# One transformer block on one core: another order, a VectorE minimum and other copies in the last attention stage

## The chip, the cores and the metric

The kernel runs on one core of one Trainium2 chip. The metric is the device time of one execution in microseconds (us). Three executions of the kernel before took 1998.77 to 1999.62 us, with a median of 1999.25 us.

Five engines have their own queue of instructions each and work through it in order: TensorE (PE in the profile, its weight loads PEld), VectorE (DVE), ScalarE (ACT), GpSimd (POOL) and SyncE (SP), which here only starts DMAs. Semaphores tie them together. TensorE writes to PSUM, which has eight banks of 128 partitions x 512 float32; VectorE and ScalarE read and write both PSUM and SBUF, and GpSimd works in SBUF.

## What is computed

The input is 2048 tokens of 512 numbers. It is normalised (layer norm without weights) to xn, and the output is x + attention(xn) + ffn(xn):

```python
xn = _layernorm(x)                       # (1, 2048, 512)
q, k, v = split(xn @ w_qkv.T)            # 16 heads of 32
scores = q @ k.T / sqrt(32)
scores = where(causal, scores, lowest)
attn = softmax(scores) @ v
x1 = attn @ w_o.T
gate, up = xn @ Wg.T, xn @ Wu.T          # 4096 wide, 4-bit weights with scales
out = x + x1 + (gelu_tanh(gate) * up) @ Wd.T
```

## The kernel before

The tokens are split into four blocks of 512 queries; `ORDER = (1, 2, 3, 0)` is the order in which they are worked on. The 16 heads make 8 pairs. All matmuls but a few are in float32.

Attention is done twice over. First, `score_rows` and `maxima` compute scores with queries on the partitions and take each query's maximum; `split` cuts the negated maximum into three bfloat16 parts. `rows_from_parts` transposes them on TensorE (L269) and ScalarE copies them, so that they lie along the free dimension. Second, `score_cols` (L288) writes the negated maxima into a PSUM tile with keys on the partitions, `add_scores` (L303) adds the scores on top, and ScalarE takes the exponential, which cannot exceed one. `attend` (L351) multiplies the exponentials with the values and with a tile of ones, so that the upper half of a PSUM bank holds the values' sum and the lower half the sum of the exponentials.

A step is one block of queries against one tile of 128 keys: 4 * qb + 4 steps for block qb, 40 for a pair (`steps`). The last four key tiles of a block are diagonal: only the columns from `c0` on are computed (512, 384, 256, 128 of them), and the first 128 of those hold scores of later keys, which may exceed the maximum. In `exponentials` ScalarE therefore takes Relu(-score) of these 128 columns into `clip` (L323), the exponential of the rest (L325), and the exponential of -clip for both heads at once (L327). Then GpSimd sets the later keys' exponentials to zero (L328). A step that is not diagonal has one exponential of 512 columns for each head (L317).

The score tiles lie in two pools of three banks, `ps_t` and `ps_s`; the last two banks, `ps_m`, hold the attended values, m0 and m1. For pairs 0 to 5 the first pass of a later pair runs along with the second pass of the present one. The loop at L552 to L574 does the last two pairs (6 and 7) together, and is the stage of this change: pair 6 uses `ps_t` and m0, pair 7 `ps_s` and m1. An iteration issues the score matmuls of both pairs for this step, then `attend` of both pairs for the step before, then the exponentials of this step. When a block is complete, `keep_attention` copies the values (ScalarE, L370) and the sums (VectorE, L371) of each pair out of PSUM, and `normalize_attention` takes one reciprocal of 128x128 on VectorE (L379) and one product on GpSimd (L381) in each of the next iterations.

The same loop prepares tokens for the feed-forward part. `token_rest` cuts a 128x512 piece of xn into a high part (a mask on VectorE, L539), a low part (a subtraction on GpSimd, L542), a mixed part (VectorE, L544, which waits for GpSimd) and the raised low part (ScalarE, L547, which waits for L544). Eight pieces (the first two blocks of `ORDER`) are done here, started after steps with an even key tile that is not diagonal.

After the loop comes the output projection (L750 to L779): 16 tiles of tokens, four matmuls each (L753), added by VectorE (L760) to x. The first tiles are those of block 1. Along with it, `token_rest` prepares the other two blocks, `token_high` (L732) rebuilds the high parts, and the first 4-bit weights are decoded. Its eight PSUM banks come from the pool `ps_f` (L589). Then the feed-forward part takes the rest of the time, up to the end.

The order on every engine is the order of the program text (`manual_schedule`); a pool's buffers come round in turn.

Of the kernel before, what the change touches and what calls it, by code (L numbers as in the profile page):

```python
# [67 lines left out]
SUM_SCALE = -TRUE / SPLIT  # L68

ORDER = (1, 2, 3, 0)  # L70

STEPS = NTB * (NTB + 1) * 2

# [2 lines left out]
def block_kernel(  # L76
# [34 lines left out]
    with (  # L111
# [199 lines left out]
        def exponentials(p, n, tiles):  # L311
            qb, kt = steps[n]
            c0 = max(0, kt - 4 * qb) * P
            prob = probs.tile([P, 2, TB], F32, tag="prob", name=f"prob{p}_{n}")
            if kt < 4 * qb:
                for h, ps in enumerate(tiles):
                    nc.scalar.activation(prob[:, h, :], ps, AF.Exp)  # L317
                return prob


            clip = clipp.tile([P, 2, P], F32, tag="clip", name=f"clip{p}_{n}")
            for h, ps in enumerate(tiles):
                nc.scalar.activation(clip[:, h], ps[:, c0 : c0 + P], AF.Relu, scale=-1.0)  # L323
# [3 lines left out]
            nc.scalar.activation(diag, clip, AF.Exp, scale=-1.0)  # L327
            nc.gpsimd.affine_select(  # L328
                out=diag,
                in_=diag,  # L330
                compare_op=ALU.is_ge,
                fill=0.0,
                base=0,
                pattern=[[0, 2], [1, P]],
                channel_multiplier=-1,
            )
            return prob

        avs, sums = {}, {}

        def attend(p, n, prob):

            qb, kt = steps[n]
            if kt == 0:
                turn[0] = (NTB * p + qb) % 2 if p < NP - 2 else p % 2
                avs[p, qb] = ps_m.tile([P, TB], F32, tag=f"m{turn[0]}", name=f"av{p}_{qb}")
            av = avs[p, qb]
            c0 = max(0, kt - 4 * qb) * P
            for h in range(4):
                head = 2 * p + h % 2  # L350
                nc.tensor.matmul(  # L351
                    av[D * h : D * (h + 1), c0:],
                    lhsT=v[kt // 4][:, kt % 4, D * head : D * (head + 1)] if h < 2 else ones,
                    rhs=prob[:, h % 2, c0:],
                    start=(kt == 0),
                    stop=(kt == 4 * qb + 3),
                )
            if kt == 4 * qb + 3:
                full.append((p, qb))

        full, invert = [], []
# [1 line left out]
        def keep_attention():  # L363

            p, qb = full.pop(0)
            av = avs[p, qb]
            og, half = p // 2, slice(64 * (p % 2), 64 * (p % 2 + 1))
            if p % 2 == 0:
                sums[og, qb] = sump.tile([P, TB], F32, tag="sums", name=f"sums{og}_{qb}")
            nc.scalar.copy(aT[og][qb][half], av[:64])  # L370
            nc.vector.tensor_copy(sums[og, qb][half], av[64:])  # L371
            if p % 2 == 1:
                invert.extend((og, qb, i) for i in range(4))

# [156 lines left out]
                        wo.append(t[:, k])  # L531


        lm = {}

        def token_rest(b, k, high):

            xk, (low, mixed) = xnT[b][:, k], lm[b, k]
            nc.vector.tensor_scalar(  # L539
                high.bitcast(I32), xk.bitcast(I32), HIGH, None, ALU.bitwise_and  # L540
# [3 lines left out]
            nc.vector.scalar_tensor_tensor(  # L544
                mixed, high, SPLIT, low.bitcast(F32), ALU.mult, ALU.subtract
            )
            nc.scalar.activation(low, low.bitcast(F32), AF.Copy, scale=1.0 / SPLIT)  # L547
            yield

        early = [(i, k) for i in range(2) for k in range(NK)]  # L550
        rest = iter(())
        for n in range(STEPS):  # L552
            rows_when_due(joint=True)
            two = [score_cols(NP - 2, n, ps_t), score_cols(NP - 1, n, ps_s)]
            for i in range(2):
                add_scores(NP - 2 + i, n, two[i])
            for _ in range(2):
                attend(*pending.pop(0))
            for i in range(2):
                pending.append((NP - 2 + i, n, exponentials(NP - 2 + i, n, two[i])))  # L560
            while full:
                keep_attention()
            if invert:
                normalize_attention()
            next(rest, None)
            qb, kt = steps[n]
            if early and kt < 4 * qb and kt % 2 == 0:
                i, k = early.pop(0)
                b = ORDER[i]
                lm[b, k] = [  # L570
                    turn_tile(8 * i + 2 * k + part, f"lm{b}_{k}_{part}", F32R)
                    for part in range(2)
                ]
                rest = token_rest(b, k, qkp.tile([P, TB], F32, tag=f"qk{k % 2}", name=f"hx{b}_{k}"))  # L574
                next(rest)
        while pending:
            attend(*pending.pop(0))
        while full:
# [7 lines left out]
    stage = ctx.enter_context(tc.tile_pool(name="stage", bufs=3, reuse_waits="tile"))  # L586
    gup = ctx.enter_context(tc.tile_pool(name="gu", bufs=4, reuse_waits="tile"))
    accp = ctx.enter_context(tc.tile_pool(name="acc", bufs=1, reuse_waits="tile"))
    ps_f = ctx.enter_context(tc.tile_pool(name="ps_f", bufs=8, space=PSUM))  # L589

    def bank(name):
        return ps_f.tile([P, TB], F32, tag="f", name=name)
# [136 lines left out]
    def token_high(b, k):  # L729

        xh[b, k] = late.tile([P, TB], F32R, tag=f"aT{k}_{b}", name=f"xh{b}_{k}")
        nc.vector.scalar_tensor_tensor(  # L732
            xh[b, k], lm[b, k][0].bitcast(F32), -SPLIT, xnT[b][:, k], ALU.mult, ALU.add
        )

    with tc.manual_schedule():

# [12 lines left out]
        for n, t in enumerate(order):  # L750
# [193 lines left out]
```

## Time and profile before

| what | value |
|---|---|
| median of three executions | 1999.25 us (1998.77 to 1999.62) |
| the profiled execution | 1999.17 us |
| its span, first to last instruction | 1997.4 us |
| TensorE busy | 1960.7 us (98%) |
| VectorE, ScalarE, GpSimd busy | 1311.8, 1105.3, 727.4 us |
| the last two pairs | from 734.4 us to about 859 us |
| output projection | 860.35 us to about 916 us |
| TensorE idle from 734 to 862 us | 128.0 - 117.6 = 10.4 us |
| mean granted clock of TensorE | 0.998 |

A row of the timeline has the start in us, the duration in us, the engine, the line of the kernel, the operation, the tile written <- the tiles read, the shape and the count; brackets give the idle time before it on its engine, and what ended it. A row of groups has the shape, the count, the busy time in us and the mean of one in ns, and the idle time before. TensorE's rows overlap, since it is pipelined and since matmuls that use 32 rows or columns run side by side; a step's cost is therefore read from start to start.

### The profile page before, as it was taken

The page shows a single profiled execution, that of the slowest core. Times are in us where ns is not written, and L with a number is a line of the kernel's source. Part 1 is how long each engine was busy: PE and PEld are TensorE (multiplying, and loading weights), DVE is VectorE, ACT ScalarE, POOL GpSimd, SP SyncE. Part 2 cuts the span into 40 slices and gives each one's busy share as a digit, 9 for nine tenths or more (in the row PEclk, how much of TensorE's full clock was granted, in tenths as well). Part 3 has the DMA queues.
Part 4 walks back from the last instruction along what each step waited for, and adds up shares of the span by engine and source line. Part 5 has one row for each costly group of instructions (what it writes and reads, how often), then busy time and mean ns, then how long its engine had stood idle before and what let it go on. Part 6 is the DMA issues. An engine that isn't in the chain of part 4 may idle for free.

```text
span 1997.4 us, 30985 instructions
## 1 busy us (share of the span) xinstructions
PE 1960.7 (98%) x11072; PEld 1162.0 (58%) x11072; DVE 1311.8 (66%) x2642; ACT 1105.3 (55%) x2361; POOL 727.4 (36%) x893
## 2 busy tenths in 40 slices
PE   7999999999999999999999999999999999999998
PEld 3433233333333322236888888888888888888886
DVE  5657665647565662177777777777777777767674
ACT  2112664546455668734666666666666666666664
POOL 1000110202111123154555555555555555555551
PEclk9999999999999999999999999999999999999999
DMA  3000000000000000030000000000000000000002
GB/s 127 0 11 11 1 2 1 1 12 1 1 1 12 1 1 2 1 107 21 23 21 21 20 21 21 20 21 18 23 18 23 18 23 18 23 18 22 19 5 85
DMA packets 55387, 39.79 MB, mean 20 GB/s; under 512 B 14784, under 2 KB 47552, under 8 KB 55232
## 3 DMA queue, kind: packets, MB, share of 16 engines
q1 hardware_dynamic: 55232, 37.81, 6.4%
q8 instruction: 87, 1.43, 0.3%
q14 instruction: 68, 0.56, 0.1%
HBM read 33.55 MB, written 4.19 MB: 19 GB/s over the span
## 4 chain that ended last, share of the span: by engine, by line
PE 95%; ACT 2%; DVE 1%; issue 1%; POOL 0%; DMA 0%; DVEq 0%; POOLq 0%; ACTq 0%
PE gu L796 24%; PE av L351 12%; PE gu L809 12%; PE pd L859 12%; PE ps_s L214 9%; PE ps_qk L170 6%; PE pd L871 6%; PE ps_t L288 4%; PE ps_t L303 3%; PE ps_v L450 3%; PE po L753 3%; ACT prob L317 1%; PE pm L269 1%; PE ptx L439 0%; DVE sums L371 0%
## 5 line engine op out<-in xcount | busy, mean ns | idle before, releaser
L796 PE MATMUL gu<-xh,gu 128*128 128x512 f32 x1024 | 403.9, 394 | 0.0
L796 PE MATMUL gu<-lm,gu 128*128 128x512 f32 x1024 | 403.7, 394 | 0.0
L238 DVE TENSOR_REDUCE tops<-ps_s 128x1 f32<-128x512 f32 x384 | 243.5, 681 | 157.5 <-PE ps_s L214 137.2
L880 DVE SCALAR_TENSOR_TENSOR acc<-pd,acc 128x512 f32<-128x512 f32 x512 | 316.8, 680 | 2.7 <-PE pd L871 2.7
L351 PE MATMUL av<-prob,v 128*32 128x512 f32 (+3 forms) x1280 | 290.5, 542 | 3.6 <-DVE sums L371 2.6
L214 PE MATMUL ps_s<-qk,qk 32*128 32x512 f32 (+3 forms) x1280 | 291.1, 576 | 0.0
L351 PE MATMUL av<-prob,ones 128*32 128x512 f32 (+3 forms) x1280 | 290.5, 542 | 0.0
L317 ACT ACTIVATE prob<-ps_t 128x512 f32<-128x512 f32 x384 | 205.8, 596 | 148.0 <-PE ps_t L303 146.6
L809 PE MATMUL gu<-lm,gu 128*128 128x512 f32 x1024 | 279.7, 395 | 0.0
L841 POOL TENSOR_TENSOR parts<-inter,hi 128x512 fp32r<-128x512 f32 x128 | 171.3, 1338 | 278.3 <-DVE hi L837 272.0
L833 DVE SCALAR_TENSOR_TENSOR inter<-gu,gate 128x512 f32<-128x512 f32 x128 | 88.5, 691 | 275.5 <-PE gu L809 274.1
L303 PE MATMUL ps_t<-qk,qk 32*128 32x512 f32 (+3 forms) x1280 | 264.2, 535 | 0.0
L866 ACT ACTIVATE pd<-pd 128x512 f32<-128x512 f32 x512 | 263.2, 580 | 1.1 <-PE pd L859 1.1
L859 PE MATMUL pd<-wd,parts 128*128 128x512 f32 x1024 | 259.6, 396 | 0.0
L803 ACT ACTIVATE gu<-gu 128x512 f32<-128x512 f32 x256 | 148.7, 581 | 188.2 <-PE gu L796 188.2
L809 PEld LDWEIGHTS gu<-lm,gu 128*128 128x128 f32 x1024 | 192.0, 188 | 47.1 <-issue 0.2
L796 PEld LDWEIGHTS gu<-lm,gu 128*128 128x128 f32 x1024 | 191.9, 187 | 46.6 <-POOL wd L677 0.2
L859 PEld LDWEIGHTS pd<-wd,parts 128*128 128x128 f32 x1024 | 192.3, 188 | 45.8
L796 PEld LDWEIGHTS gu<-xh,gu 128*128 128x128 f32 x1024 | 192.0, 188 | 45.7 <-ACT wd L676 0.2
L328 POOL TENSOR_SCALAR_AFFINE_SELECT prob<-prob 128x256 f32<-128x256 f32 x128 | 52.1, 408 | 423.3 <-ACT prob L327 376.7
L233 DVE CUSTOM_DVE_ANT_0 ps_s<-ps_s,mask_qk 128x128 f32<-128x128 f32 (+3 forms) x256 | 120.7, 516 | 101.5 <-PE ps_t L303 55.8
L840 ACT CAST parts<-hi 128x512 fp32r<-128x512 f32 x128 | 79.8, 623 | 172.9 <-DVE hi L837 172.9
(91 smaller groups left out, 2684.9 us busy)
## 6 DMA issues: line engine op xcount, KB each, us to landing
pk<-packed SPq DMA_DIRECT2D x96, 128.0 KB, 2.2
sc<-scales SPq DMA_DIRECT2D x512, 8.0 KB, 1.6
x<-x SPq DMA_DIRECT2D x16, 256.0 KB, 4.1
acc<-x SPq DMA_DIRECT2D x16, 256.0 KB, 3.2
sc<-scales SPq DMA_DIRECT2D x256, 16.0 KB, 1.7
out<-acc SPq DMA_DIRECT2D x16, 256.0 KB, 2.2
wqk<-w_qk SPq DMA_DIRECT2D x4, 512.0 KB, 3.6
wv<-w_v SPq DMA_DIRECT2D x4, 256.0 KB, 6.1
```

The source lines that it names most:

```text
L214: nc.tensor.matmul(ps[:, :w], lhsT=qT[p // 2, qb][rows, i * P : (i + 1) * P], rhs=kT[p // 2, c][rows, :w], start=True, stop=True,)
L238: nc.vector.tensor_reduce(top, ps[:, :w], AX.X, ALU.max)
L303: nc.tensor.matmul(ps[:, c0:], lhsT=kT[p // 2, kt // 4][rows, (kt % 4) * P : (kt % 4 + 1) * P], rhs=qT[p // 2, qb][rows, c0:], start=False ...
L317: nc.scalar.activation(prob[:, h, :], ps, AF.Exp)
L351: nc.tensor.matmul(av[D * h : D * (h + 1), c0:], lhsT=v[kt // 4][:, kt % 4, D * head : D * (head + 1)] if h < 2 else ones, rhs=prob[:, h % ...
L796: nc.tensor.matmul(ps, lhsT=parts[:, i, k], rhs=mov, start=(k == 0 and i == 0), stop=(k == NK - 1 and i == 1),)
L803: nc.scalar.activation(ps, ps, AF.Copy, scale=HIGH_SCALE)
L809: nc.tensor.matmul(ps, lhsT=gu[g, m, j][:, 2, k], rhs=lm[b, k][1], start=False, stop=(k == NK - 1), skip_group_check=True,)
L841: nc.gpsimd.tensor_tensor(parts[:, 1], inter, high, ALU.subtract)
L859: nc.tensor.matmul(po, lhsT=parts[:, part, i * P : (i + 1) * P], rhs=w[:, part], start=(part == 0), stop=(part == 1),)
L866: nc.scalar.activation(po, po, AF.Copy, scale=HIGH_SCALE)
L880: nc.vector.scalar_tensor_tensor(acc[t], po, SUM_SCALE, acc[t], ALU.mult, ALU.add)
```

## The change

It does six things, the first four of them in the stage of the last two pairs.

1. The order of the steps in this stage: the blocks come in the order 1, 0, 2, 3 (`TOGETHER`), and in block qb each of the four diagonal steps is followed by qb others. Which matmul starts and which ends a block's sum is handed to `attend`.
2. Diagonal steps: VectorE limits the 128 diagonal columns at zero, in place in PSUM, and then one exponential for each head covers all columns. The Relu and the separate exponential of the diagonal go. The zeroing on GpSimd stays.
3. When a block is complete, ScalarE copies both halves of pair 6, and VectorE both halves of pair 7.
4. Tokens of the first two blocks are prepared after even steps whose next step is not diagonal.
5. The raised low part of the tokens is taken out of `token_rest`. For the first two blocks it is made in the output projection, after the high part, which is now xn minus the unraised low part. For the other two it is issued after the mixed part as before.
6. `ps_f` gets `reuse_waits="tile"`: each of its banks waits for the earlier tiles in that place rather than for the earlier pools.

The core of the diff:

```diff
+TOGETHER = (1, 0, 2, 3)
...
-            nc.scalar.copy(aT[og][qb][half], av[:64])
-            nc.vector.tensor_copy(sums[og, qb][half], av[64:])
+            if p < NP - 2:
+                nc.scalar.copy(aT[og][qb][half], av[:64])
+                nc.vector.tensor_copy(sums[og, qb][half], av[64:])
+            else:
+                copy = nc.scalar.copy if p % 2 == 0 else nc.vector.tensor_copy
+                copy(aT[og][qb][half], av[:64])
+                copy(sums[og, qb][half], av[64:])
...
+        together = []
+        for qb in TOGETHER:
+            mine = [n for n in range(STEPS) if steps[n][0] == qb]
+            for d in range(4):
+                together += [mine[4 * qb + d], *mine[d * qb : (d + 1) * qb]]
...
+        def exponentials_together(p, n, tiles):
+            if not diagonal(n):
+                return exponentials(p, n, tiles)
+            qb, kt = steps[n]
+            c0 = (kt - 4 * qb) * P
+            prob = probs.tile([P, 2, TB], F32, tag="prob", name=f"prob{p}_{n}")
+            for h, ps in enumerate(tiles):
+
+                nc.vector.tensor_scalar(
+                    ps[:, c0 : c0 + P], ps[:, c0 : c0 + P], 0.0, None, ALU.min
+                )
+                nc.scalar.activation(prob[:, h, c0:], ps[:, c0:], AF.Exp)
+            omit_later_keys(prob[:, :, c0 : c0 + P])
+            return prob
...
-            nc.scalar.activation(low, low.bitcast(F32), AF.Copy, scale=1.0 / SPLIT)
...
-        for n in range(STEPS):
+        for s, n in enumerate(together):
...
-            qb, kt = steps[n]
-            if early and kt < 4 * qb and kt % 2 == 0:
+            if early and s % 2 == 0 and not diagonal(together[s + 1]):
...
-    ps_f = ctx.enter_context(tc.tile_pool(name="ps_f", bufs=8, space=PSUM))
+    ps_f = ctx.enter_context(
+        tc.tile_pool(name="ps_f", bufs=8, space=PSUM, reuse_waits="tile")
+    )
...
+        low = lm[b, k][0].bitcast(F32)
+        if b in ORDER[:2]:
+            nc.vector.tensor_tensor(xh[b, k], xnT[b][:, k], low, ALU.subtract)
+            multiply_low(b, k)
...
+    def multiply_low(b, k):
+        low = lm[b, k][0]
+        nc.scalar.activation(low, low.bitcast(F32), AF.Copy, scale=1.0 / SPLIT)
...
-            next(tokens, None)
+            if n in range(1, 9):
+                next(tokens)
+                multiply_low(ORDER[2 + (n - 1) // NK], (n - 1) % NK)
```

More of the change, by code (lines that the diff above doesn't have):

```diff
@@ L327, in exponentials, with omit_later_keys @@
             nc.scalar.activation(diag, clip, AF.Exp, scale=-1.0)
+            omit_later_keys(diag)
+            return prob
+        def omit_later_keys(diag):
             nc.gpsimd.affine_select(
@@ L336, in exponentials, with attend @@
             )
-            return prob
         avs, sums = {}, {}
-        def attend(p, n, prob):
+        def attend(p, n, prob, first=None, last=None):
             qb, kt = steps[n]
-            if kt == 0:
+            if first is None:
+                first, last = kt == 0, kt == 4 * qb + 3
+            if first:
                 turn[0] = (NTB * p + qb) % 2 if p < NP - 2 else p % 2
@@ L354, in attend @@
                     rhs=prob[:, h % 2, c0:],
-                    start=(kt == 0),
-                    stop=(kt == 4 * qb + 3),
+                    start=first,
+                    stop=last,
                 )
-            if kt == 4 * qb + 3:
+            if last:
                 full.append((p, qb))
@@ L531, in block_kernel, with diagonal @@
                         wo.append(t[:, k])
+        together = []
[3 more added lines that the diff above has]
+                together += [mine[4 * qb + d], *mine[d * qb : (d + 1) * qb]]
+        def diagonal(n):
+            return steps[n][1] >= 4 * steps[n][0]
+        def exponentials_together(p, n, tiles):
[10 more added lines that the diff above has]
+            omit_later_keys(prob[:, :, c0 : c0 + P])
+            return prob
         lm = {}
@@ L558, in block_kernel @@
                 attend(*pending.pop(0))
+            qb = steps[n][0]
+            ends = [
+                s == 0 or steps[together[s - 1]][0] != qb,
+                s == STEPS - 1 or steps[together[s + 1]][0] != qb,
+            ]
             for i in range(2):
-                pending.append((NP - 2 + i, n, exponentials(NP - 2 + i, n, two[i])))
+                prob = exponentials_together(NP - 2 + i, n, two[i])
+                pending.append((NP - 2 + i, n, prob, *ends))
             while full:
@@ L575, in block_kernel @@
                 next(rest)
+        assert not early
         while pending:
@@ L731, in token_high @@
         xh[b, k] = late.tile([P, TB], F32R, tag=f"aT{k}_{b}", name=f"xh{b}_{k}")
-        nc.vector.scalar_tensor_tensor(
-            xh[b, k], lm[b, k][0].bitcast(F32), -SPLIT, xnT[b][:, k], ALU.mult, ALU.add
-        )
+        low = lm[b, k][0].bitcast(F32)
+        if b in ORDER[:2]:
+            nc.vector.tensor_tensor(xh[b, k], xnT[b][:, k], low, ALU.subtract)
+            multiply_low(b, k)
+        else:
+            nc.vector.scalar_tensor_tensor(
+                xh[b, k], low, -SPLIT, xnT[b][:, k], ALU.mult, ALU.add
+            )
+    def multiply_low(b, k):
+        low = lm[b, k][0]
+        nc.scalar.activation(low, low.bitcast(F32), AF.Copy, scale=1.0 / SPLIT)
     with tc.manual_schedule():
```

## The prediction, made before the changed kernel was run

> **What bounds the kernel now.** First the page: busy shares, clock row and the chain that ended last.
>
> ```profile
> PE 1960.7 (98%) x11072; PEld 1162.0 (58%) x11072; DVE 1311.8 (66%) x2642; ACT 1105.3 (55%) x2361; POOL 727.4 (36%) x893
> ...
> PEclk9999999999999999999999999999999999999999
> ...
> PE 95%; ACT 2%; DVE 1%; issue 1%; POOL 0%; DMA 0%; DVEq 0%; POOLq 0%; ACTq 0%
> ```
>
> TensorE is busy 98% of the span and carries 95% of the chain, so a microsecond in which it stands still is a microsecond of the kernel; only 1997.4 - 1960.7 = 36.7 us are idle. The clock row rounds, so I cut the span into stretches and looked at the stage that the change touches (the last two pairs, 734.4 to 860.35 us) in pieces of 5 us. Columns: busy time with counts for each engine, then the granted clock.
>
> ```profile
> core 0: us, PE busy (x) PEld busy (x) DVE busy (x) ACT busy (x) POOL busy (x), PEclk, DMA share, GB/s
> 825.00:830.00 5.00, 5.00 (x52) 1.57 (x52) 0.00 (x0) 2.96 (x7) 0.00 (x0) 1.00 0.00 2
> 845.00:850.00 5.00, 2.81 (x40) 1.09 (x36) 0.96 (x2) 4.30 (x14) 1.22 (x3) 0.99 0.01 3
> 850.00:855.00 5.00, 5.00 (x40) 1.30 (x39) 3.82 (x5) 2.94 (x14) 1.60 (x4) 0.67 0.00 0
> 855.00:860.00 5.00, 3.19 (x52) 1.04 (x44) 1.10 (x2) 4.33 (x15) 2.52 (x7) 1.00 0.20 54
> 860.00:865.00 5.00, 4.66 (x7) 2.08 (x8) 3.68 (x5) 1.07 (x2) 1.82 (x4) 0.66 0.90 293
> ```
>
> At 825 TensorE is full. At 845 and 855 it loses 2.2 and 1.8 us, and the pieces after each run at a clock of 0.67: in pieces of 1 us this is half clock from 849.9 and from 860.4, 3.4 us each. Then the timeline of TensorE alone, for what a step costs and what it waits for.
>
> ```profile
> 758.93 0.40 PE L288 MATMUL ps_t<-neg,ones_h 3*128 3x512 bf16 x4
> ...
> 760.70 0.62 PE L288 MATMUL ps_t<-neg,ones_h 3*128 3x512 bf16 x3
> 761.90 0.37 PE L288 MATMUL ps_t<-neg,ones_h 3*128 3x512 bf16 x1 [0.59 <-ACT prob L317]
> ...
> 763.57 0.62 PE L351 MATMUL av<-prob,v 128*32 128x512 f32 x2 [0.43 <-DVE sums L371]
> ...
> 768.46 0.38 PE L288 MATMUL ps_t<-neg,ones_h 3*128 3x512 bf16 x1
> ...
> 770.18 0.37 PE L288 MATMUL ps_t<-neg,ones_h 3*128 3x512 bf16 x1 [0.58 <-ACT prob L317]
> ...
> 773.20 0.39 PE L288 MATMUL ps_t<-neg,ones_h 3*128 3x512 bf16 x4
> ...
> 776.24 0.40 PE L288 MATMUL ps_t<-neg,ones_h 3*128 3x512 bf16 x4
> ```
>
> A step of this stage is: score rows (L288, L303) for both pairs, then the values and sums (L351, "attend") of the step before. 773.20 to 776.24 is an undisturbed full step: 3.04 us. At 758.93 the attend starts 1.19 us later (760.12, next rows), so scores take 1.19 and a full attend 1.86. Narrow ones, from the same rows elsewhere: attends of 384, 256, 128 columns 1.43, 1.05, 0.58; scores 0.89, 0.65, 0.57. "x3 ... x1 <-ACT" is the score ring: three banks for a pair, two used in a step, so the fourth L288 needs the third Exp of the step before. Subtracting undisturbed durations from the start-to-start times of all 40 steps gives what the stage loses:
> - entry, 734.41 to 741.46: 0.5 + 1.5 = 2.0
> - Exps queued behind the raise of a token's low part (L547), which waits for VectorE, which waits for GpSimd (744.5, 768.5, 805.0): 1.0 + 1.7 + 1.7 = 4.4
> - a full step after a 128-column attend, then its attend waiting for the sum copy (760.70 to 765.42, again at 797): 1.7 + 1.7 = 3.4
> - diagonal steps waiting for the zeroing (L328), blocks 1 to 3: 2.0
> - block 0 at the end: 846.13 to 853.40 takes 7.27 for 2.75 of work, of which 1.7 is the half clock; with its last step 5.1
> - last attends done at 858.2, first output matmul at 860.35: 2.15, waiting for the sums
> - half clock after it, 3.4 us at half speed: 1.7
>
> Sum 20.7 us, the most that any order of this stage can give back.
>
> ```profile
> 860.35 3.98 PE L753 MATMUL po<-wo,aT 128*128 128x512 f32 x5 [1.45 <-DVE sums L371]
> ```
>
> **Part by part.** *ScalarE in diagonal steps.* Costs from the groups of this stage by shape:
>
> ```profile
> L317 ACT ACTIVATE prob<-ps_t 128x512 f32<-128x512 f32 x96 | 49.5, 601 | 15.6 <-PE ps_t L303 15.6
> ...
> L323 ACT ACTIVATE clip<-ps_t 128x128 f32<-128x128 f32 x64 | 17.6, 287 | 5.1 <-PE ps_t L303 4.5
> ...
> L327 ACT ACTIVATE prob<-clip 128x256 f32<-128x256 f32 x32 | 14.1, 442 | 0.7
> ...
> L547 ACT ACTIVATE lm<-lm 128x512 fp32r<-128x512 f32 x8 | 5.1, 644 | 7.4 <-DVE lm L544 7.4
> ...
> L233 DVE CUSTOM_DVE_ANT_0 ps_s<-ps_s,mask_qk 128x128 f32<-128x128 f32 x1 | 0.3, 295 | 0.0
> ```
>
> 64 Relus and 32 wide Exps go (17.6 + 14.1 us), and 48 narrow Exps (19.6) become 64 wider ones. In a row, an Exp advances ScalarE 0.515 us for 512 columns (2.06 for four), about 0.40, 0.29 and 0.16 for 384, 256, 128; a diagonal step of 512 columns drops from 3.0 (two pairs from 728.86 to 730.37, 1.5 each) to 2.06, below TensorE's 3.04.
>
> *VectorE's minimum, added.* 64 instructions, 128x128, PSUM to PSUM: not in the trace. Nearest row: the masked maximum above, also 128x128 in PSUM, two inputs: 295 ns. I take 0.29 us, bounds 0.2 and 0.45. [...]
>
> *Queue behind the minimum.* The built order shows VectorE's queue: minima, then reciprocals (0.93), mask (0.36) and the product waiting for GpSimd's 1.26. In most places a full step lies between and the queue is empty in time. In the entry it isn't: sum copy 739.9, two reciprocals, mask and product end at 743.5, so the second diagonal's Exps start 0.7 late (0.5 us of ring wait). In block 0 a reciprocal waits for ScalarE's copies ahead of the minima.
>
> *Raise moved out.* 8 x 0.64 us leave ScalarE here, the 4.4 us go, and come back in the output projection, where ScalarE was busy 15.7 of 50 us: nothing, as long as TensorE runs at its own pace there. High parts as a subtraction (0.68, row of L760) instead of 0.78: nothing.
>
> *Order.* TensorE's own work is unchanged. A full step after a diagonal now follows an attend of 384, 256 or 128 columns. Its third Exp ends 1.19 + 0.07 + 1.65 + 0.07 = 2.98 after its start, the next fourth L288 is reached 0.16 after the next step begins, at 2.62, 2.24, 1.77: waits 0.2, 0.58, 1.05 (the trace has this last one: 760.86 to 761.90). 1.83 per block, three blocks: 5.5, less 0.2 already in the entry: 5.3. The 3.4 and 2.0 of the ledger go.
>
> *Block 0 second.* I chain it from the durations. Last full step of block 1; diagonal 0: its Exps end 2.45 after its scores, then two copies on ScalarE, 1.19; the attend of diagonal 0 waits 0.85 for them. VectorE's reciprocal waits for the copies too, the minima of diagonal 1 follow it, ring wait 0.8. Diagonals 2 and 3: nothing. Block 2's first full step meets a 128-column attend and minima (1.38), and block 0's copies (0.6). Sum 3.65. Block 2 to 3: copies, 0.65. Copying each pair's two halves on one engine saves little: 1.19 on ScalarE against 0.58 + 0.69 in turn. The entry: 0.5 + 1.2 + 0.6 + 0.5 = 2.8; a transpose in the ring 0.2.
>
> *End.* The last step is full; its last attend runs straight into the first output matmul, which no longer waits for a whole pool: the built order shows the second projection waiting for VectorE's copies (1.4 us) behind 3.3 us of the first. 2.15 and 1.7 go. If that cover were gone, 1.4 comes back. VectorE starts the projection 2 to 3 us later against TensorE; it idled 10.2 us there for L760, so nothing.
>
> *Half clock.* [...] By the row, about 2.2 us idle in pieces within 3.4 cost 3.4 us at half clock, twice. I take the row. Block 0's new place loses at most about 1.4 idle us in such a stretch; I expect no half clock.
>
> After: 2.8 + 5.3 + 3.65 + 0.65 + 0.2 = 12.6. Gain 20.7 - 12.6 = 8.1; chaining start to start gave 7.9. I take 7.9. The profiled execution took 1999.17 (span 1997.4 and 1.8 around it), the median of the runs shown is 1999.25: 1999.2 - 7.9 = 1991.3.
>
> **Rivals.**
> - *As worked out*, 1991.3, own range 1989 to 1994: 0.55.
> - *More comes back*: the ring waits (5.3) overlap with others, 1.5 to 4 us better: 1988. For it: they are estimates of one row; against: that row is exact. 0.10.
> - *Half clock in block 0's new place and minima at 0.45*: 1.7 + 4 x 0.5 in block 0 and entry, + about 0.3: 4.0 less gain, 1995.3. For it: three waits close together. 0.17.
> - *It doesn't do what it says*: what TensorE gains up to 860 is waited for in the projection, VectorE late by 3 to 5 us at the first gate matmul: 1998.5. Against: 10.2 us of VectorE's waiting there. 0.10.
> - *Slower*: the minimum in PSUM is dear. With M per minimum, the third Exp ends about 3M + 0.17 + 0.45 after the scores, and the fourth L288 is due at 2.02; 12 diagonals lose 12 x (3M - 1.40), so the gain is eaten from M = 0.69 us. At 0.9, 12 x 1.3 = 15.6, less 7.9: 2006.9. Against: 0.295 in the nearest row. 0.08.
>
> **Numbers.** A measurement of this kernel tells about 0.2% (4 us) from no change. Below 1995.2: first two, and half of the third, and more as its size varies: 0.76; within: 0.14; slower: 0.10. Range 1988 to 1997: it leaves out the slow case, half of the fourth and a little below.
>
> **What would show it.** Right: no Exp queued behind a raise of low parts in this stage; no clock under 1 between 700 and 920; the first output matmul at about 852 to 856 with no wait; minima at 0.25 to 0.35; ring waits of about 0.6 and 1.0 after the third and fourth diagonals. Wrong: minima over 0.6; half clock near block 0; TensorE waiting for VectorE between 860 and 920; a stage that still ends near 860.

## The result and the profile after

The changed kernel takes 1991.95 us (median of 7 runs, 1990.40 to 1993.41), the kernel before, in the same comparison, 1998.77 us (7 runs, 1996.33 to 1999.62). The ratio is 0.9968, 95% interval 0.9956 to 0.9979: faster by 0.3%. The prediction was 1991.3 us, range 1988 to 1997. The profiled execution of after took 1993.41 us, its span is 1991.7.

The page of after, busy time of the engines and the shares of the chain that ended last:

```profile
PE 1958.1 (98%) x11072; PEld 1163.9 (58%) x11072; DVE 1326.4 (67%) x2706; ACT 1092.6 (55%) x2281; POOL 727.3 (37%) x893
...
PE 96%; ACT 2%; DVE 1%; issue 1%; DMA 0%; POOL 0%; DVEq 0%; SPq 0%; ACTq 0%; POOLq 0%
```

TensorE still sets the time. VectorE does 64 instructions more, ScalarE 80 fewer. The end of the changed stage, in the stretches shown of before (busy time with counts for each engine, then the granted clock):

```profile
core 0: us, PE busy (x) PEld busy (x) DVE busy (x) ACT busy (x) POOL busy (x), PEclk, DMA share, GB/s
845.00:850.00 5.00, 4.41 (x52) 1.51 (x48) 0.00 (x0) 2.59 (x7) 0.88 (x3) 1.00 0.00 2
850.00:855.00 5.00, 5.00 (x48) 1.37 (x47) 0.00 (x0) 3.92 (x8) 0.00 (x0) 1.00 0.00 0
855.00:860.00 5.00, 5.00 (x24) 1.99 (x17) 3.27 (x5) 2.77 (x5) 0.50 (x2) 1.00 0.28 65
860.00:865.00 5.00, 5.00 (x13) 2.28 (x12) 3.87 (x7) 0.03 (x1) 2.59 (x4) 1.00 0.64 198
```

The clock is 1.00 throughout; both half clocks of before (3.4 us each) are gone, and TensorE idles 0.6 us in these 20 us. The stage, from its first score row to the first output matmul, ran from 734.41 to 860.35 before (125.94 us, one half clock of 3.4 us in it) and runs from 736.16 to 856.47 now (120.31 us). What is left in it, and its end, from the timeline of TensorE:

```profile
757.89 0.40 PE L290 MATMUL ps_t<-neg,ones_h 3*128 3x512 bf16 x4
...
759.65 0.62 PE L290 MATMUL ps_t<-neg,ones_h 3*128 3x512 bf16 x3
760.86 0.37 PE L290 MATMUL ps_t<-neg,ones_h 3*128 3x512 bf16 x1 [0.59 <-ACT prob L319]
...
763.88 0.55 PE L290 MATMUL ps_t<-neg,ones_h 3*128 3x384 bf16 x4
...
765.69 0.62 PE L358 MATMUL av<-prob,v 128*32 128x512 f32 x2 [0.61 <-POOL prob L334]
...
795.18 0.39 PE L290 MATMUL ps_t<-neg,ones_h 3*128 3x512 bf16 x3
795.96 0.37 PE L290 MATMUL ps_t<-neg,ones_h 3*128 3x512 bf16 x1 [0.39 <-ACT prob L319]
...
856.47 5.85 PE L806 MATMUL po<-wo,aT 128*128 128x512 f32 x13
```

The lines of before have moved: score rows L290, attend L358, Exp of a full tile L319, Exp of a diagonal L566, minimum L563, zeroing L334. "x3" and then "x1 <-ACT prob L319" is the ring wait, the wait for a free bank of the score ring. The step at 757.89 lasts only 1.76 us, since it attends a diagonal of 128 columns; the next one, at 759.65, comes to its fourth score row before the third Exp of the step at 757.89 is done. So it lasts 4.23 us, to 763.88, for 3.04 of work. The bracket shows only 0.59, since the ends of the rows ahead are modelled; the loss is read from start to start. At 765.69 the attend of block 0's first diagonal waits; the bracket names the zeroing, which had ended at 765.09, while ScalarE's copy of the sums ended at 765.59. The output matmul at 856.47 has no bracket: it starts when the last attend is done.

ScalarE's and VectorE's groups of this stage, by shape (busy time and mean of one in ns, then the idle time before them and who ended it):

```profile
L319 ACT ACTIVATE prob<-ps_t 128x512 f32<-128x512 f32 x96 | 49.6, 603 | 24.1 <-PE ps_t L305 24.0
...
L563 DVE TENSOR_SCALAR ps_t<-ps_t 128x128 f32<-128x128 f32 x64 | 14.3, 292 | 45.6 <-PE ps_t L305 45.2 <-ACT neg L274 0.3
L566 ACT ACTIVATE prob<-ps_t 128x512 f32<-128x512 f32 x16 | 8.3, 603 | 5.4 <-DVE ps_t L563 4.0 <-POOL negm L258 1.4
```

A minimum's own time is 292 ns on average, four in a row take 0.89 us. Of the 5.4 us that ScalarE idles ahead of the widest diagonal Exps, 4.0 end with a minimum; a full tile's Exps wait for scores alone. Subtracting undisturbed steps as the prediction did, the stage loses 13.9 us now: entry 3.2, ring waits 6.4 (in each of blocks 2 and 3, 0.33, 0.76 and 1.18 us after diagonals of 384, 256 and 128 columns; 0.64 and 1.19 behind those of block 1), block 0 3.67, block 2 to block 3 0.67.

Where the 5.7 us of span went: the stage 5.63 shorter, what follows it 1.85 shorter, and the part ahead of it 1.75 longer, by a half clock at 194.5 in a part of the program that the change does not touch (last section). Of the 1.85, 1.6 are in the output projection, which lost the half clock at 860: from its first matmul to the first gate matmul it took 56.2 us before and 54.6 now, and no row of TensorE between 856 and 925 has a bracket. What the stage gained is not waited for there.

### The profile page after: what moved, and what is told of

It reads as the page before. It is cut to its first block, busy times and chain, and to the rows that moved or that the text cites. A ratio compares the mean times of both kernels' runs of the same rounds, so it can differ in the third digit from the quotient of the medians.

```text
span 1991.7 us, 31028 instructions
## 1 busy us (share of the span) xinstructions
PE 1958.1 (98%) x11072; PEld 1163.9 (58%) x11072; DVE 1326.4 (67%) x2706; ACT 1092.6 (55%) x2281; POOL 727.3 (37%) x893
## 4 chain that ended last, share of the span: by engine, by line
PE 96%; ACT 2%; DVE 1%; issue 1%; DMA 0%; POOL 0%; DVEq 0%; SPq 0%; ACTq 0%; POOLq 0%
PE gu L851 24%; PE av L358 12%; PE gu L864 12%; PE pd L914 12%; PE ps_s L216 9%; PE ps_qk L172 6%; PE pd L926 6%; PE ps_t L290 4%; PE ps_t L305 3%; PE ps_v L462 3%; PE po L806 3%; ACT prob L319 1%; PE pm L271 1%; PE ptx L451 0%; ACT prob L566 0%
## 5 line engine op out<-in xcount | busy, mean ns | idle before, releaser
L319 ACT ACTIVATE prob<-ps_t 128x512 f32<-128x512 f32 x384 | 205.9, 597 | 158.1 <-PE ps_t L305 156.7
L358 PE MATMUL av<-prob,v 128*32 128x512 f32 (+3 forms) x1280 | 288.6, 540 | 2.0 <-issue 0.7
L358 PE MATMUL av<-prob,ones 128*32 128x512 f32 (+3 forms) x1280 | 288.5, 541 | 0.0
L334 POOL TENSOR_SCALAR_AFFINE_SELECT prob<-prob 128x256 f32<-128x256 f32 x128 | 52.2, 409 | 424.2 <-ACT prob L329 317.4
```

The lines of the kernel that those rows point to most:

```text
L358: nc.tensor.matmul(av[D * h : D * (h + 1), c0:], lhsT=v[kt // 4][:, kt % 4, D * head : D * (head + 1)] if h < 2 else ones, rhs=prob[:, h % ...
```

## Experiments

**Theories.** By the prediction, each loss of before goes with one part of the change: the waits at narrow steps and block 0 with the new order, queued Exps with the raise, the end with the pool; the ring waits are the price of the order. The rival: ScalarE's relief by the minima carries the rest, and without it the new order doesn't work. Each experiment was run beside the kernel before, and the ratios are against it. These were three comparisons, each on another chip, and the kernel before had medians of 1996.86 us in the first (experiments 1 to 4), 1999.12 in the second (5 to 7) and 1999.46 in the third (8 to 11). So medians of different rows are not set against each other to a microsecond. The effects are read from the stage, in one trace of each kernel; an undisturbed full step takes 3.04 us in all of them. "Clean" is the stage less 1.7 us for each half clock of 3.4 us inside it.

| kernel | median us (runs) | ratio, 95% | stage us | clean |
|---|---|---|---|---|
| before | 1998.77 (7) | 1 | 125.94 | 124.2 |
| after | 1991.95 (7) | 0.9968, 0.9956 to 0.9979 | 120.31 | 120.3 |
| exponentials alternate | 1988.95 (5) | 0.9958, 0.9944 to 0.9971 | 116.23 | 116.2 |
| raise kept | 1992.77 (11) | 0.9979, 0.9971 to 0.9988 | 121.30 | 121.3 |
| pool waits | 1994.56 (11) | 0.9983, 0.9974 to 0.9992 | 122.11 | 122.1 |
| minima twice | 2003.82 (5) | 1.0034, 1.0021 to 1.0046 | 130.89 | 127.5 |
| Relus kept | 1993.34 (8) | 0.9971, 0.9961 to 0.9981 | 120.52 | 120.5 |
| copies divided | 1995.63 (11) | 0.9981, 0.9972 to 0.9990 | 123.17 | 121.5 |
| before + minima | 1997.24 (11) | 0.9992, 0.9983 to 1.0000 | 125.38 | 123.7 |
| before + block 0 second | 1998.31 (11) | 0.9999, 0.9990 to 1.0008 | 125.42 | 123.7 |
| after, old order | 1988.76 (5) | 0.9945, 0.9932 to 0.9957 | 117.19 | 115.5 |
| after, block 0 last | 1991.71 (5) | 0.9965, 0.9951 to 0.9978 | 120.07 | 120.1 |
| alternate, full step first | 1989.78 (5) | 0.9952, 0.9940 to 0.9965 | 117.12 | 117.1 |
| alternate, no minima | 1990.13 (5) | 0.9954, 0.9942 to 0.9967 | 118.74 | 117.0 |

**1. The exponentials of the two pairs alternate** (pair 6 tile 0, pair 7 tile 0, pair 6 tile 1, pair 7 tile 1), so that the fourth score row needs the second Exp, not the third.

```
-            for i in range(2):
-                prob = exponentials_together(NP - 2 + i, n, two[i])
+            both = exponentials_both(n, two)
...
+            for h in range(2):
+                for i in range(2):
+                    ps = two[i][h]
...
+                    nc.scalar.activation(both[i][:, h, c0:], ps[:, c0:], AF.Exp)
```

> The exponentials of the two pairs alternate (pair 6 head 0, pair 7 head 0, pair 6 head 1, pair 7 head 1), minima likewise; nothing else differs from the changed kernel. The score-ring theory: the fourth score-row matmul then needs the second exponential of the step before, not the third, so each ring wait shrinks by one exponential, 0.515 us: after the diagonals of 384, 256, 128 columns from about 0.33, 0.76, 1.18 to 0, 0.25, 0.67, in three blocks 4.0 us, with the entry about 4.5. The stage, from its first score row to the first output matmul, goes from 120.3 to about 116, the median from 1992 to about 1987.5. The rival, that these waits are ScalarE's rate in a row of steps and not one bank: the order of its work changes nothing, stage 120, median 1992.

Measured: the stage is 4.1 us shorter; the theory had about 4.3. The timeline of TensorE in this kernel, at the same step as 803.04 in after (4.22 us there):

```profile
800.40 1.09 PE L290 MATMUL ps_t<-neg,ones_h 3*128 3x512 bf16 x4
...
804.14 0.39 PE L290 MATMUL ps_t<-neg,ones_h 3*128 3x512 bf16 x4
```

All four rows go without a bracket, and the step lasts 3.74 us. Steps after 384 and 256 columns last 3.04 (3.37 in after) and 3.31 (3.80). So most of the ring waits came from the order of the Exps, and they were real cost. After 128 columns 0.7 us stays.

**2. The raise of the low parts stays in the stage** (that part undone; the high parts, too, are rebuilt as before, which the lines below leave out).

```
                 mixed, high, SPLIT, low.bitcast(F32), ALU.mult, ALU.subtract
             )
+            if b in ORDER[:2]:
+                nc.scalar.activation(low, low.bitcast(F32), AF.Copy, scale=1.0 / SPLIT)
             yield
```

> The changed kernel with the raise of the low parts of the first two blocks back in the attention stage, and their high parts rebuilt as before. The queue theory: a raise waits for VectorE's product, which stands behind reciprocals and GpSimd's subtraction, and exponentials queue behind it, above all where reciprocals are due: in the entry (0.6 to 1.5) and at the full step after block 0 (about 2.3); the other six are in time and cost nothing. Stage 120.3 + 3.5 = 123.8 (2.5 to 4.5 more), median about 1995.5. The rival, that 8 x 0.64 us more of ScalarE's time is hidden because TensorE needs more time in a step: no difference.

Measured: 1.0 us of stage, between the two, and far from the 4.4 us that the raise cost before. ScalarE's row and the score row that waits behind it, in this kernel:

```profile
780.51 0.63 ACT L585 ACTIVATE lm<-lm 128x512 fp32r<-128x512 f32 x1 [1.71 <-DVE lm L581]
781.05 2.04 ACT L319 ACTIVATE prob<-ps_t 128x512 f32<-128x512 f32 x4
```

```profile
782.65 0.32 PE L290 MATMUL ps_t<-neg,ones_h 3*128 3x384 bf16 x1 [0.61 <-ACT prob L319]
```

It is the only bracket of the stage that after lacks. The other raises stand ahead of Exps that a narrow step would make wait anyhow: at 747.25 the ring wait is 0.37 us against 0.33 without the raise.

**3. The pool of the output projection waits as a whole** (that part undone).

```
-        tc.tile_pool(name="ps_f", bufs=8, space=PSUM, reuse_waits="tile")
+        tc.tile_pool(name="ps_f", bufs=8, space=PSUM)
```

> The changed kernel with the projection's PSUM pool waiting for whole pools again. The theory: the first output matmul then waits for VectorE's second copy of the last block, which ends at about 858.0 where the matmul starts at 856.47: stage 120.3 + 1.6 = 121.9, median about 1993.5, and no half clock, since TensorE is busy up to that gap. The rival: block 0 in another place alone removed the 2.15 us at the end, and the pool's wait changes nothing. A third outcome: the gap of 1.6 us brings half clock, and the median is 1995.

Measured: 1.8 us of stage (1.6 expected by the theory). The wait stands at the first output matmul of this kernel:

```profile
857.80 2.38 PE L806 MATMUL po<-wo,aT 128*128 128x512 f32 x5 [1.72 <-DVE sums L383]
```

**4. Each minimum is done twice** (same values).

```
+                for _ in range(2):
+                    nc.vector.tensor_scalar(
...
```

> The changed kernel with every minimum done twice (same values). The theory: 64 more instructions of 0.29 us, four in a row measured 0.89; the first exponential of a diagonal step starts 0.22 later, the third tile's minimum is done 1.35 us after the scores, still within the ring's 1.8 to 2.0 us. What is lost is 0.2 to 0.3 at each 512-column diagonal and 0.3 to 0.5 in block 0 and at the entry: stage 120.3 + 2 (1 to 3), median about 1994. The rival of the prediction, that the minimum lies on the path: the added 18.7 us of VectorE show up in large part, at least 8 us more.

Measured: 10.6 us of stage, 3.4 of them two half clocks, 7.2 waits; all five runs took longer than the kernel before. The rows of VectorE, here and in after (one row each):

```profile
778.41 2.23 DVE L564 TENSOR_SCALAR ps_t<-ps_t 128x128 f32<-128x128 f32 x8 [0.23 <-PE ps_t L305]
```

```profile
762.09 0.89 DVE L563 TENSOR_SCALAR ps_t<-ps_t 128x128 f32<-128x128 f32 x4 [1.36 <-PE ps_t L305]
```

A pair of minima on the same tile takes 2.23 / 4 = 0.56 us, so this is M = 0.56 in the prediction's terms. Stretches of 3.41 us before and in the two half clocks of this kernel:

```profile
736.91:740.32 3.41, 2.44 (x32) 0.84 (x28) 2.09 (x8) 1.95 (x4) 1.44 (x6) 1.00 0.00 0
740.32:743.73 3.41, 3.41 (x17) 0.67 (x16) 2.52 (x4) 2.47 (x6) 1.20 (x3) 0.50 0.00 0
777.87:781.28 3.41, 2.03 (x31) 0.69 (x27) 3.02 (x10) 1.89 (x4) 1.17 (x3) 1.00 0.01 2
781.28:784.69 3.41, 3.41 (x17) 0.88 (x20) 2.79 (x5) 2.81 (x7) 1.39 (x3) 0.50 0.02 5
```

My 1 to 3 us were far too low. The rival's 8 us or more is reached with the half clocks, and nearly so without them. It would pay to make minima cheaper only if they cost something at 0.22 us each; the next one asks that.

**5. Relus kept**: the new order and everything else, but no minima.

```
-                prob = exponentials_together(NP - 2 + i, n, two[i])
+                prob = exponentials(NP - 2 + i, n, two[i])
```

> The changed kernel with its new order, but with the limiting at zero left on ScalarE as before (Relu, wide Exp, Exp of the negated part) and no minima. Theory (the order carries the gain, the minima only a little): a diagonal step of 512 columns costs ScalarE 3.0 us against a cover of 3.04, the narrower ones stay under theirs, so only block 0, whose four diagonals follow each other, and the entry lose: stage 120.3 + 1 to 3 = 121.3 to 123.3 us, total about +1 to +3 us on the changed kernel. Rival (relieving ScalarE is what makes the new order work): at least 6 us of the stage come back, 126 us or more, and the total is that of the kernel before or longer.

Measured: 0.2 us of stage. Among runs with a mean granted clock of 1.000, one of this kernel took 1990.74 us and three of after 1990.40 to 1990.62. ScalarE's groups in this stage:

```profile
L325 ACT ACTIVATE clip<-ps_t 128x128 f32<-128x128 f32 x66 | 18.0, 287 | 7.9 <-PE ps_t L305 7.7
...
L329 ACT ACTIVATE prob<-clip 128x256 f32<-128x256 f32 x34 | 15.0, 441 | 0.9 <-POOL prob L334 0.4
```

With 19.8 us of wide Exps (L327) the diagonals take ScalarE 52.8 us, some 27 more than in after, VectorE 14.3 less, and the stage is as long: in most steps both ways fit under TensorE. The rival falls. The +1 to 3 us that I expected did not come either: four steps lose 0.4 us more each than in after (the second, block 0's second, the first full ones of blocks 2 and 3), but the fourth step and block 0's third lose 0.7 less each, and the ring waits a little less.

**6. Copies divided as before** (ScalarE the values, VectorE the sums of each pair).

```
-            if p < NP - 2:
+            if True:
                 nc.scalar.copy(aT[og][qb][half], av[:64])
```

> The changed kernel, but the copies of values and sums of the last two pairs divided as before: ScalarE the values, VectorE the sums, for each pair. Theory (copying each pair on one engine saves little, 1.19 us on ScalarE against 0.58 and 0.69 in turn): stage 120.3 within 0.5 us, total within 0.6 us of the changed kernel. Rival (the copies are what the first attend of the next block waits for, two engines at once matter): 0.5 to 0.7 us more at each of three block ends, and 1 us at the end of the stage, together 2 us or more.

Measured: 2.9 us of stage, 1.7 of it a half clock, 1.2 waits. The rival is right that the copies matter; its 1 us at the end of the stage did not come (the last step and the end take 4.75 us in both). TensorE's rows in block 0 and where block 2 begins, and the stretches at the second:

```profile
768.17 0.28 PE L290 MATMUL ps_t<-neg,ones_h 3*128 3x256 bf16 x2 [0.40 <-ACT prob L566]
...
777.63 0.76 PE L358 MATMUL av<-prob,v 128*32 128x512 f32 x2 [0.52 <-DVE sums L379]
```

```profile
774.57:777.98 3.41, 2.22 (x16) 0.68 (x18) 1.34 (x3) 3.36 (x8) 0.81 (x2) 1.00 0.00 0
777.98:781.39 3.41, 3.41 (x24) 0.85 (x20) 2.65 (x5) 1.47 (x3) 2.05 (x3) 0.50 0.02 5
```

The sum copy on VectorE is what the attend waits for again at three block ends, for 0.79, 0.52 and 0.52 us; after has waits of 0.61, 0.34 and 0.34 in these places. The larger part, 0.7 us, comes one step later in block 0: VectorE's second sum copy ends 6.80 us after that block's first step began, where after's last copy ends at 5.94, and the reciprocal, the minima and the Exp that the row at 768.17 waits for stand behind it. The half clock follows the second of these block ends, a stretch with 2.22 us of busy TensorE in 3.41.

**7. One part alone, twice.** Kernel before with minima only, and kernel before with block 0 second only.

```
+            if p >= NP - 2:
+                for h, ps in enumerate(tiles):
+                    nc.vector.tensor_scalar(
+                        ps[:, c0 : c0 + P], ps[:, c0 : c0 + P], 0.0, None, ALU.min
+                    )
+                    nc.scalar.activation(prob[:, h, c0:], ps[:, c0:], AF.Exp)
...
```

> The kernel before with one part only: in the last two pairs VectorE limits the diagonal scores at zero in PSUM and one Exp a tile follows. Order, copies, raise and pool as before. Theory: ScalarE gets 12 us shorter in the diagonals, so most of the 2.0 us of waiting for the zeroing in blocks 1 to 3 and 1 to 2 us of block 0 at the end go, the rest stays: stage 125.9 - 2 to 4 = 122 to 124 us, total -2 to -4. Rival (in the old order the minima queue behind reciprocals and mask products, and behind each other in four diagonals in a row): stage within 1 us of 125.9 or longer. The half clock at the end stays by both.

```
-        for n in range(STEPS):
+        early_n = [n for qb in (1, 0, 2, 3) for n in range(STEPS) if steps[n][0] == qb]
+        for n in early_n:
```

> The kernel before with one part only: in the last two pairs block 0 comes second instead of last; within each block the order is as before (diagonals at its end). Theory: block 0's loss (5.1 us at the end, 1.7 of it half clock) becomes about 3 to 4 without a half clock, and the stage ends with the diagonals of block 3 in its place, whose narrow attends still leave the first output matmul waiting about 2 us for the sums: stage 125.9 - 1 to 3 = 123 to 125 us. Rival (the end costs the same whichever diagonals stand there): within 0.7 us of 125.9, half clock before the output projection included.

Measured: 0.5 us of stage each; both intervals of the ratio reach 1. Both rivals hold: block 0 costs about the same in either place, half clock included, and minima alone leave the queued raises, the sum copies and the end nearly as they were. In the trace with minima alone the stage's half clock stands at 806, and there is none at 850 or 860; my expectation had it stay at the end.

**8. The changed kernel in the old order**: full steps first, then the four diagonals, blocks 1, 2, 3, 0; minima, copies, raise and pool as changed. With the order goes its fourth point, the places at which tokens are prepared.

```
-TOGETHER = (1, 0, 2, 3)
+TOGETHER = (1, 2, 3, 0)
...
-            for d in range(4):
-                together += [mine[4 * qb + d], *mine[d * qb : (d + 1) * qb]]
+            together += mine
...
-            if early and s % 2 == 0 and not diagonal(together[s + 1]):
+            if early and not diagonal(n) and steps[n][1] % 2 == 0:
```

> The changed kernel with the order of steps of before: in each block the full steps first, then its four diagonals, blocks 1, 2, 3, 0; minima, copies, raise and pool as changed. Theory (the parts add up): undoing copies, raise and pool one at a time took 1.2 (without the half clock that came with it), 0.9 and 1.8 us back and minima alone gave 0.5, together 4.4 of the 5.6 us that the stage became shorter, so the order itself is worth about 1.2 and the stage is 121 to 122 us here. Rival (the order is what lets the other parts work: minima alone and block 0 second alone gave 0.5 us each): the stage is 124 us or more, with half clocks at block 0.

Measured: 117.19 us of stage, 3.1 less than after, with a half clock that after doesn't have; all five runs (1986.38 to 1989.16) lie below all seven of after, though the kernel before was no faster in this comparison (1999.46) than in that one (1998.77). Both expectations were too high: the order, the most visible part of the change, costs time. Order and token places were not undone one without the other; but the waits that the new order has and this one lacks are mostly ring waits behind full tiles' Exps, and in neither kernel does ScalarE do token work in this stage. TensorE's rows in this kernel, at the place where a raise stood in before (805.00) and at block 0:

```profile
801.57 0.39 PE L290 MATMUL ps_t<-neg,ones_h 3*128 3x512 bf16 x4
...
804.61 0.39 PE L290 MATMUL ps_t<-neg,ones_h 3*128 3x512 bf16 x4
...
841.96 0.32 PE L290 MATMUL ps_t<-neg,ones_h 3*128 3x384 bf16 x1 [0.64 <-ACT prob L565]
...
843.54 1.07 PE L358 MATMUL av<-prob,v 128*32 128x512 f32 x2 [0.61 <-POOL prob L334]
```

From 801.57 to 804.61 is an undisturbed step, 3.04 us, where before lost 1.7. Step by step against before: the three raise steps give 4.4 us back, the end 2.1, the diagonal steps that waited for zeroings and a full step ahead of them 1.0, block 0's first steps 0.8, the sum copies 0.45; together 8.8, for 125.94 - 117.19 = 8.75. Only one full step in each block follows a 128-column attend; in after nearly every diagonal is followed by a step that waits.

**9. The changed kernel with block 0 last.**

```
-TOGETHER = (1, 0, 2, 3)
+TOGETHER = (1, 2, 3, 0)
```

> The changed kernel with block 0 last again (blocks 1, 2, 3, 0), diagonals spread in the others. Theory (the prediction's ledger: block 0 5.1 us at the end with a half clock against 3.65 second, and the first output matmul waiting about 1.5 us for the last sums, whose wait is no longer covered by a full step): stage 120.3 + 2 to 4 = 122.3 to 124.3 us. Rival (where block 0 stands is worth nothing, as moving it alone gave 0.5 us): within 1 us of 120.3.

Measured: 120.07 us, within 0.3 of after; the rival holds. Its end, from TensorE's timeline:

```profile
853.86 0.30 PE L358 MATMUL av<-prob,v 128*32 128x128 f32 x2 [0.44 <-POOL prob L334]
...
854.60 3.70 PE L806 MATMUL po<-wo,aT 128*128 128x512 f32 x8
```

Narrow attends stand at the end and the output matmul follows without a wait: with experiment 3, it is the pool, not the full step at the end, that takes the wait away.

**10. Alternating exponentials, with a full step ahead of the first diagonal** in blocks 2 and 3 (the lines of experiment 1 are left out).

```
+            if qb > 1:
+                first = len(together) - len(mine)
+                together[first : first + 2] = together[first + 1], together[first]
```

> The kernel with alternating exponentials, and in blocks 2 and 3 the first full step ahead of the first diagonal. There the first attend of blocks 2 and 3 waits 0.83 and 0.59 us for the zeroing of a diagonal of 512 columns, which comes after minima and the copies of the block before. Theory: a full step has neither minima nor zeroing, both waits go: stage 116.2 - 1.0 to 1.5 = 114.7 to 115.2 us, total about 1987.7 us. Rival (the copies of the block before are what is late, and the wait stays with them, or moves to the diagonal one step later): stage within 0.4 us of 116.2.

Measured: 117.12, 0.9 longer than with alternation alone. TensorE's two first attends wait like this now:

```profile
773.29 0.62 PE L358 MATMUL av<-prob,v 128*32 128x512 f32 x2 [0.79 <-ACT sums L383]
...
807.53 0.62 PE L358 MATMUL av<-prob,v 128*32 128x512 f32 x2 [0.20 <-ACT sums L383]
```

These two steps got 0.46 and 0.38 us shorter and the steps after them 0.62 and 0.81 longer: the copies are late by themselves, and the rest of the wait moved one step on. That is the rival's mechanism, at more than its 0.4 us.

**11. Alternating exponentials in full steps only, no minima.**

```
-            both = exponentials_both(n, two)
+            if diagonal(n):
+                both = [exponentials(NP - 2 + i, n, two[i]) for i in range(2)]
+            else:
+                both = exponentials_both(n, two)
```

> The kernel with alternating exponentials in its full steps only: diagonal steps keep ScalarE's Relu, wide Exp and Exp of the negated part, pair after pair, and there are no minima. Theory (minima are worth next to nothing in this order, 0.2 us of stage when taken out of the changed kernel, and the alternation carries the gain): stage 116.2 + 0.5 to 1.5 = 116.7 to 117.7 us. Rival (once the ring waits are gone the diagonals' ScalarE time is the next bound): stage 119 us or more.

Measured: 118.74, of which 1.7 is a half clock at 740.8; 117.0 without it, 0.8 above the kernel with minima, as the theory expected. The half clock follows two waits in the entry:

```profile
738.31 0.37 PE L290 MATMUL ps_t<-neg,ones_h 3*128 3x512 bf16 x1 [0.93 <-ACT prob L327]
...
740.59 0.90 PE L358 MATMUL av<-prob,v 128*32 128x512 f32 x2 [1.04 <-DVE sums L379]
```

In the 3.41 us ahead of it TensorE is busy for 1.46. With minima (experiment 1) there is one wait of 1.17 us here, 2.25 us are busy, and no half clock follows. The ratios of the two kernels (0.9954 and 0.9958) do not tell them apart.

## Why the prediction was right, and where its steps failed

**The total** was right: 1991.95 for 1991.3. That the medians meet within 0.7 us is in part luck: the median fell by 6.8 us for the 7.9 forecast, from a kernel before that took 1998.77 in this comparison and 1999.25 when the prediction was made, and the runs of one kernel lie up to 3 us apart. The traces are the better test. From the first score row to the first gate matmul they gained 7.2 us (5.63 and 1.6) where the prediction had 7.9. In its ledger, 125.94 and the 1.7 after it less 20.7 leave 106.9 us of undisturbed work, so it expected a stage of 119.5; 120.31 was measured.

**Right by their own working.** No Exp queues behind a raise; no clock below 1 from 700 to 920; the output matmul starts at 856.47 without a wait (852 to 856 had been given, for a stage that starts 1.75 earlier); minima at 292 ns (0.29); block 0 second loses 3.67 (3.65); block 2 to 3 0.67 (0.65). The 64 small instructions on VectorE hardly count in this stage: four minima on four tiles advance it by 0.22 us each (0.89 in all), and leaving all 64 out moves the stage 0.2 us (experiment 5). How long minima hold the Exps back, which block 0's chain needs (Exps done 2.45 us after the scores), no row of before shows; in after, the first minimum of block 0's first diagonal starts at 762.09, the first Exp at 762.49, 0.40 later, and the last Exp ends at 764.55, 2.46 after the minimum's start.

**Sizes off.** The ring waits were 0.33, 0.76 and 1.18 where 0.2, 0.58 and 1.05 had been worked out, in all 6.4 for 5.3: the third Exp ended 0.13 to 0.18 later than its chain of rows said. The entry lost 3.2 for 2.8.

**The step that failed: who gives what.** "The 3.4 and 2.0 of the ledger go" stood under the order, and block 0's 5.1 with it. The order does take the 3.4 away (2.9 of it stays in the old order with the other parts), but for 6.4 of its own; the zeroings lose up to 1.0 less in the old order too, and block 0's place is worth 0.5 us or less. The part of the ledger that belongs to no order was there to be summed: 4.4 for the raise, 2.15 for the end and 2.0 for the zeroing from 125.94 make 117.4, and experiment 8 measured 117.19 (closer than the terms deserve: the zeroings gave 1.0, and block 0's steps and the sum copies the rest). With its own expected stage of 119.5, the prediction already held the new order to be a loss of 2 us, and did not say so; it is 3.1, or 4.8 between clean stages.

**The raise** was worth 4.4 us in the old order (steps of 4.33, 4.74 and 4.75 us became 3.37, 3.04 and 3.04; with minima alone they stay at 4.3 or more; the raise alone was not moved in the old order) and 1.0 in the new one. The savings did not add here: an Exp that was late behind a raise cost next to nothing where the next score row waited for an earlier diagonal anyhow (0.37 against 0.33 us at 747.25).

**The copies** "save little" was wrong: 1.2 us of waits and a half clock. The prediction summed the engines' time (1.19 against 0.58 and 0.69), and neither which copy the next attend waits for nor what stands behind the copies in VectorE's queue.

**The end**: "its last attend runs straight into the first output matmul" holds, but by the pool alone: a full step at the end without it still waits 1.72 (experiment 3), and narrow ones with it do not wait for the sums (experiment 9). Not all of the 2.15 was that wait: the bracket at 860.35 has 1.45, the last attends were done at 858.9 and not at 858.2, and they had waited for the zeroing.

**The rival "slower"** put the point at which the minimum eats the gain at M = 0.69 us. At 0.56 (experiment 4) its formula, 12 x (3 x 0.56 - 1.40), gives 3.4 us; 7.2 of waits and 3.4 of half clock were measured, and the kernel was slower than before. The formula took each diagonal alone; in block 0 a minimum also stands behind reciprocals (0.94 us each), and it left the clock out. How much each of the two adds was not taken apart. The break-even lies between 0.22, the same measure of the changed kernel, and 0.56.

**Open.** The old order with alternating exponentials, which the results point to, was not run; each alone shortens after's stage, by 3.1 and 4.1 us. Whether the projection gives some of the stage's time back in single kernels was not taken apart further.

## What to carry to other kernels

When a change has several parts, sum the ledger once without each part, the most visible one above all: here the new order cost 3 us and rode on parts that needed no order. Where a ring of buffers makes a step wait for the k-th product of the step before, first change which product frees the needed buffer (alternate the producers), before moving steps. A narrow step gave little cover to the full step behind it: spread, each of them made a full step wait here (0.33 to 1.18 us), gathered, mainly the last one did (1.45 us, with the sum copies).

## What the runs showed of the hardware

Half clocks, stretches of 3.41 us in which the granted clock is 0.50, sit on a grid in the four traces below. In before they start at 849.89, 860.13 and 1996.77: 3 and 333 times 3.413 us apart; in the kernel with doubled minima 740.32 and 781.28 are 12 apart, in that with block 0 second alone 765.94 and 861.52 are 28 apart, in after 194.48 and 1989.9 are 526. The last ones of before and after are cut short by the end of the span. The prediction's reading of its rows, about 2.2 us idle in pieces ahead of each half clock, was 2.19 and 1.92 in the two stretches of the grid (busy 1.22 of 3.41 from 846.48, 1.49 from 856.72). In this stage and at its end, ten stretches of the grid, over all the traces, with 1.22 to 2.47 us of busy TensorE in 3.41 were followed by half clock, and no single wait before one was over 1.45 us. These records give no sharp limit: of the stretches with 2.0 to 2.5 us busy some were followed by half clock and some not (2.22 us in experiment 6 was, 2.14 in experiment 9 was not), one of 1.69 us (experiment 3) was not, and none above 2.5 was.

The grid's place differs from run to run, and the same waits came with a half clock in one run and without in the next. The stretches around 194 us, ahead of anything that the change touches, in before and then in after (busy time of TensorE alone, then the granted clock):

```profile
190.00:194.00 4.00, 2.27 (x21) 1.00 0.40 131
194.00:198.00 4.00, 4.00 (x35) 1.00 0.03 6
```

```profile
190.00:194.00 4.00, 2.27 (x23) 1.00 0.38 131
194.00:198.00 4.00, 4.00 (x23) 0.57 0.00 0
```

Busy time is 2.27 us in both; only after fell to half clock, 0.57 on average over the second stretch; 3.41 us at half clock are worth 1.7, and the stage of after starts 1.75 later. Cut at each run's own grid, the stretch ahead of that point differs, 2.09 us of busy TensorE in before and 1.86 in after:

```profile
191.12:194.53 3.41, 2.09 (x19) 1.00 0.25 99
```

```profile
191.07:194.48 3.41, 1.86 (x15) 1.00 0.27 109
```

This fits the runs of after, which stand in groups some 2 us apart (1990.4 to 1990.6 at a mean clock of 1.000, 1991.95 to 1993.4 at 0.999). It is not all that differs between runs: with no half clock ahead of it, the stage starts at 733.08 us in the trace of the kernel before with minima and at 734.60 in that of experiment 8, behind the same code. This is why stages are compared here by the trace.

Two minima in a row on one tile take 0.56 us, on different tiles 0.22 each, where one by itself takes 0.29: two on the same tile come within 0.02 us of twice the 0.29 (0.58), while on different tiles each comes 0.07 sooner. That the second reads what the first wrote is the author's reading of it; no run here shows the reason.
